# A router's gate in pairs of tiles, its statistics in the scan before it, and eight key projections moved

## The chip, the cores and the metric

The kernel runs on one core of a Trainium2 chip. A core has five engines that each work through a list of instructions in order and wait for each other on semaphores: TensorE (PE; its weight loads are shown apart as PEld), VectorE (DVE), ScalarE (ACT), GpSimd (POOL) and SyncE (SP, which here only issues transfers). Data lie in SBUF, with 128 partitions; matmuls write to eight banks of PSUM; transfers between SBUF and the large memory run on 16 DMA engines. The metric is the device time of one execution in microseconds (us).

## The reference

Four sequences of 512 tokens with 512 features (`x`) and a context of 256 features pass through four stages, each added to `x`:

```python
x = x + ssm(ctx, layernorm(x))       # selective scan over the context, gated by silu of the normed x
x = x + moe(layernorm(x))            # 64 experts, 8 chosen per token
x = x + xattn(layernorm(x), ctx)     # 16 heads; queries from x, keys and values from ctx
x = x + bitlinear_ffn(layernorm(x))  # ternary weights, 8-bit activations
```

The change concerns the scan's end, the router of the experts, and the attention's keys. The router and the keys are

```python
probs = softmax(xn @ gate_weight.T)                 # 2048 tokens x 64 experts
top_val, top_idx = top_k(probs, 8)                  # first 4 primary, last 4 secondary
# experts that are only ever secondary are replaced by a similar primary one
mapping = where(replace, best_primary, arange(64))
...
k = rmsnorm((ctx @ Wk).reshape(B, 512, 16, 128), gk)
```

The keys depend on the context alone, so their 64 tasks (4 sequences x 16 heads) can be done at any time before the attention.

## The kernel before

The 2048 tokens are 16 tiles of 128 (`NT` = 16); four tiles (`NC` = 4) are one sequence b. `x_all` stays in SBUF all the time. The program has three parts, one after the other.

**The recurrence** (`ssm_phase`). `seq` has 128 slots: b, then feature chunk c (4), then pairs of states i (8). In a slot, POOL makes `dBu` two slots ahead (`inputs(q + 2)`, three buffers), ACT makes the decay `dA` one slot ahead (in PSUM, apart from two slots per sequence that `ahead_ends` makes early in SBUF), DVE runs the scan over 1024 columns (L534), and the product with `cb` (L535) is on POOL for i = 0, 2, 4 and on DVE for the others. PE transposes the products into `yT`. In the slot with i = 2, `result` gates the previous chunk (DVE, L574) and POOL adds it to `x_all` (L576). While sequence b is scanned, `ahead` and `ahead_ends` prepare b + 1; in the last sequence there is nothing to prepare. Value projections and part of the key tasks fill PE (`values`, `key_steps`). For each sequence `stats` and `norm` (L388 to L401) compute the layernorm of that stage.

**The experts' part** (`moe_phase`) starts with `route`. Steps are put into a `Plan` with hand-set times; `run` emits them in order of time, and each engine executes its own in the order of emission. For each tile: `stats` (DVE bn_stats and bn_aggr, then four POOL instructions, L158 to L167), `norm` (ACT, L174, and a store of `xn` to memory, SP), `turn` (four PE transposes, L181), `take` (ACT copy, L186). For each pair of tiles: `logits` (eight PE instructions, L193), `turn_logits` (ACT copy L199, two PE transposes L202), `exps` (DVE maxima L207, ACT exponentials L212). Then per tile `mask` (DVE: top 8, marks; SP stores z) and `count` (PE, L909 and L914). After all tiles: `mapping` (DVE), `remap`, `ranks`, `code` and `decode` for each half of the tiles, `onehots` and `tokens` for each tile (DVE, ACT, PE), `to_places`. `PACE` = 2.7 gives each tile its place in the plan. The tiles of one pool share SBUF with tiles of pools that are closed, so a first use can wait for the last reader of what lay there.

Then `Experts.run` works through 64 experts (blocks of at most 352 rows, largest first): POOL issues the gathers of rows and weights two experts ahead, PE transposes the rows, multiplies by the gate and up weights (L1235) and the down weights (L1259 to L1269). `key_tasks` has a list of key tasks that are done one per expert from the third expert on, and `slot_tasks` and `Ternary.tasks` put other work between.

**The attention and the last stage** (`attend`) read what the others left in memory.

A key task (`Keys`) is `task` (four PE instructions of 128x512), `evict` (ACT: squares L1144 and a scaled copy L1145, SP stores the copy), `squares` (eight PE matmuls with one column, L1155) and `take` (ACT, L1167, SP stores 2 KB). Before the change the recurrence does tasks of all sequences, the experts 17, the attention 16:

```python
left = [(b, h) for b in (2, 3) for h in (6, 7)] + [(1, h) for h in range(3, H)]   # L1352
```

`load` in `Keys` brings `Wk` for eight heads to the tile `k_w` with two transfers of 512 KB, into the place that is called "hid" in the pool `late`.

Of the kernel before, what the change touches and what calls it, by code (L numbers as in the profile page):

```python
# [29 lines left out]
P = 128  # L30
# [3 lines left out]
CTX = 256  # L34
# [102 lines left out]

class Gate:
# [5 lines left out]
    def __init__(self, cm, x_all, w, dr, const, work, turned, psum):  # L144
        self.cm, self.x_all, self.dr = cm, x_all, dr
        self.work, self.turned, self.psum = work, turned, psum
# [8 lines left out]
    def stats(self, t):  # L155
        nc = self.nc
        sts = self.work.tile([P, 6], F32, name="g_st")
        nc.vector.bn_stats(sts, self.x_all[:, t, :])  # L158
        mv = self.work.tile([P, 2], F32, name="g_mv")
        nc.vector.bn_aggr(mv, sts)  # L160
        ve = self.work.tile([P, 1], F32, name="g_ve")
        nc.gpsimd.tensor_scalar(ve, mv[:, 1:2], EPS, None, ALU.add)
        rstd = self.work.tile([P, 1], F32, name="g_rstd")
        nc.gpsimd.tensor_tensor(rstd, ve, self.cm.half, ALU.pow)
        nmr = self.work.tile([P, 1], F32, name="g_nmr")
        nc.gpsimd.tensor_tensor(nmr, mv[:, 0:1], rstd, ALU.mult)
        nc.gpsimd.tensor_scalar(nmr, nmr, -1.0, None, ALU.mult)  # L167
        self.s[t] = rstd, nmr

    def norm(self, t):  # L170
        nc = self.nc
        rstd, nmr = self.s[t]
        xn = self.s[t] = self.work.tile([P, DM], F32, name="g_xn")
        nc.scalar.activation(xn, self.x_all[:, t, :], AF.Identity, bias=nmr, scale=rstd)  # L174
        nc.sync.dma_start(self.dr["xn"][t * P:(t + 1) * P, :], xn)
# [20 lines left out]
    def turn_logits(self, t):  # L196
# [3 lines left out]
        pl = self.s["pl"] = self.turned.tile([P, 2, E], F32, name="g_pl")  # L200
# [31 lines left out]
def ssm_phase(ctx, cm, x_all, w, kv, dr):  # L232
# [393 lines left out]
    def key_bank(shape, name):  # L626
        return ps.tile(shape, F32, name=name, tag=keys.banks[name == "kpss"])

    keys = Keys(cm, w, kv, small, lambda n: pool[1].tile([P, S], F32, name=f"k_{n}",
                                                         tag={"sq": "e", "kT": "wt"}[n]),  # L630
# [84 lines left out]
    for q, (b, c, i) in enumerate(seq):  # L715
# [21 lines left out]
        if i == late:  # L737
            gate(b, c)
        if q % 8 == 2 and q + 8 < len(seq):
            load_wv(q // 2 + 4)  # L740
# [32 lines left out]
def moe_phase(ctx, cm, x_all, w, kv, dr, out):  # L773
# [18 lines left out]
    with ExitStack() as es:  # L792
        more = es.enter_context(tc.tile_pool(name="b_more", bufs=1))
        keys = Keys(cm, w, kv, es.enter_context(tc.tile_pool(name="b_small", bufs=2)), None, None,
                    None)
# [1528 lines left out]
```

## Time and profile before

| | |
|---|---|
| runs (us) | 2739.28, 2743.82, 2743.28; median 2743.28 |
| profiled execution (us) | 2741.18, of which the instructions' span is 2738.4 |
| mean granted PE clock | 0.957 of full |
| busy of the span | PE 92%, DVE 55%, ACT 45%, POOL 43% |

| stage | from, to (us) |
|---|---|
| recurrence, to the last addition to `x_all` | 0 to 577.1 |
| gate of the 16 tiles: first norm, to the start of mapping | 581.5 to 649.1 |
| mapping to the first rows on PE | 649.1 to 697.8 |
| experts | 697.8 to about 1453 |
| attention and last stage | to 2738.4 |

The profile is of one execution. Its page gives the busy time of each engine, the same in 40 equal slices, the DMA queues, and the chain of work that ended last, followed back from the last instruction. Further views are asked from the trace: windows (busy time of each engine in a stretch, with the number of instructions in brackets and the granted PE clock, where 1.00 is full speed), waits (who waited for whom), and the timeline (start, duration, engine, line, operation, output<-inputs, and in square brackets the idle time before, with what ended it). PEclk in tenths and windows show the clock that was granted to PE, not a share of use.

### The profile page before, as it was taken

The page shows a single profiled execution, that of the slowest core. Times are in us where ns is not written, and L with a number is a line of the kernel's source. Part 1 is how long each engine was busy: PE and PEld are TensorE (multiplying, and loading weights), DVE is VectorE, ACT ScalarE, POOL GpSimd, SP SyncE. Part 2 cuts the span into 40 slices and gives each one's busy share as a digit, 9 for nine tenths or more (in the row PEclk, how much of TensorE's full clock was granted, in tenths as well). Part 3 has the DMA queues.
Part 4 walks back from the last instruction along what each step waited for, and adds up shares of the span by engine and source line. Part 5 has one row for each costly group of instructions (what it writes and reads, how often), then busy time and mean ns, then how long its engine had stood idle before and what let it go on. Part 6 is the DMA issues. An engine that isn't in the chain of part 4 may idle for free. (4 is left out here: it accounts for less than half of the span.)

```text
span 2738.4 us, 29994 instructions
## 1 busy us (share of the span) xinstructions
PE 2524.7 (92%) x10158; PEld 1429.8 (52%) x10158; DVE 1514.4 (55%) x2570; ACT 1239.3 (45%) x2355; POOL 1188.5 (43%) x1121
## 2 busy tenths in 40 slices
PE   5979797976899999999997899999999999999997
PEld 2545454643455656666674454445555554555543
DVE  5897979856332234334423555556665666554445
ACT  5666666643223322232322344444555555555543
POOL 3888888951333344444434433223332333211112
PEclk8989898987899999999998999999999999999999
DMA  6253535323556567889866443333432343222100
GB/s 245 90 194 109 196 117 180 116 85 104 183 180 201 175 211 224 268 273 342 298 223 206 122 143 113 96 94 122 127 100 77 116 127 112 70 81 64 52 31 20
DMA packets 198543, 403.11 MB, mean 147 GB/s; under 512 B 30563, under 2 KB 72099, under 8 KB 194288
## 3 DMA queue, kind: packets, MB, share of 16 engines
q1 hardware_dynamic: 155758, 247.76, 27.2%
q0 software_dynamic: 40576, 153.19, 18.0%
q8 instruction: 83, 1.36, 0.2%
q14 instruction: 76, 0.62, 0.1%
q10 hardware_dynamic: 2050, 0.18, 0.1%
HBM read 319.13 MB, written 81.92 MB: 146 GB/s over the span
## 5 line engine op out<-in xcount | busy, mean ns | idle before, releaser
L1889 DVE TENSOR_REDUCE mx<-psc 128x1 f32<-128x512 f32 x256 | 176.7, 690 | 457.5 <-PE psc L1886 453.8
L1235 PE MATMUL pg<-xT,wg 128*128 128x284 f32 (+12 forms) x1536 | 400.3, 405 | 1.6 <-ACT xT L1222 1.1
L1235 PEld LDWEIGHTS pg<-xT,wg 128*128 128x128 f32 x1536 | 282.9, 194 | 82.1 <-issue 33.6
L509 POOL TENSOR_TENSOR dBu<-bb,du 128x1024 f32<-128x1024 f32 x128 | 314.1, 2474 | 21.4 <-DVE dA L534 13.5
L1892 ACT ACTIVATE e<-psc,mx 128x512 f32<-128x512 f32 x256 | 176.1, 688 | 310.2 <-DVE mx L1889 309.9
L1886 PE MATMUL psc<-kT,qT 128*128 128x512 f32 x512 | 266.5, 602 | 1.0 <-ACT qT L1880 1.0
L1176 POOL DMA_INDIRECT xg<-xn_dram,tok x168 | 171.0, 1018 | 218.9 <-PE pt L1219 176.5
L1913 PE MATMUL po<-eT,v 128*128 128x512 f32 x512 | 234.9, 602 | 10.7 <-ACT eT L1907 10.7
L1852 PE MATMUL pq<-Wq,xnT 128*128 128x512 f32 x512 | 233.6, 599 | 0.7 <-ACT xnT L1811 0.7
L1922 PE MATMUL px<-Wo,oT 128*128 128x512 f32 x512 | 230.2, 593 | 0.0
L520 ACT ACTIVATE dA<-delta,negA 128x512 f32<-128x512 f32 x256 | 176.8, 694 | 81.1 <-DVE hc L535 71.0
L1906 PEld LDWEIGHTS pet<-ident,e 128*128 128x128 f32 x1024 | 127.1, 141 | 145.7 <-issue 118.8
L1863 POOL TENSOR_SCALAR qms<-qms 128x4 f32<-128x4 f32 x64 | 24.5, 382 | 411.3 <-DVE qms L1861 410.5
L534 DVE TENSOR_TENSOR_SCAN dA<-dA,dBu 128x1024 f32<-128x1024 f32 x80 | 182.8, 2284 | 24.1 <-POOL dBu L509 18.6
L1280 DVE COPY yo<-po 128x512 f32<-128x512 f32 x68 | 47.0, 691 | 230.6 <-PE po L1269 230.6
L540 PEld LDWEIGHTS yT<-ident,hc 128*128 128x128 f32 x1024 | 125.2, 149 | 92.9 <-issue 53.0
L540 PE MATMUL yT<-ident,hc 128*128 128x128 f32 x1024 | 140.6, 287 | 35.6 <-POOL hc L535 20.3
L1913 PEld LDWEIGHTS po<-eT,v 128*128 128x128 f32 x512 | 97.3, 192 | 139.1 <-issue 117.7
L1776 POOL DMA_INDIRECT yg<-y_dram,pos x124 | 125.4, 1011 | 87.2 <-issue 63.7
L1906 PE MATMUL pet<-ident,e 128*128 128x128 f32 x1024 | 154.5, 274 | 6.9 <-DVE e L1898 6.8
L1176 POOL DMA_INDIRECT wd<-down,widx x64 | 63.5, 993 | 215.6 <-PE po L1269 181.6
L1907 ACT COPY eT<-pet 128x512 f32<-128x512 f32 x256 | 148.2, 579 | 4.6 <-PE pet L1906 4.5
(352 smaller groups left out, 4475.6 us busy)
## 6 DMA issues: line engine op xcount, KB each, us to landing
y_dram<-yo SPq DMA_DIRECT2D x110, 256.0 KB
bb<-bc_dram SPq DMA_DIRECT2D x16, 1024.0 KB
cb<-bc_dram SPq DMA_DIRECT2D x16, 1024.0 KB
v_dram<-v SPq DMA_DIRECT2D x64, 256.0 KB
k_dram<-k_kT SPq DMA_DIRECT2D x64, 256.0 KB
Wq<-Wq SPq DMA_DIRECT2D x16, 1024.0 KB
kT<-k_dram SPq DMA_DIRECT2D x64, 256.0 KB
rk<-r_dram SPq DMA_DIRECT2D x64, 256.0 KB
```

The costliest lines, as they stand in the source:

```text
L509: nc.gpsimd.tensor_tensor(dBus[q], st[b]["bb"][i // 2][:, j:j + 2, :], st[b]["du"][c].unsqueeze(1).to_broadcast([P, 2, S]), ALU.mult)
L520: nc.scalar.activation(dAs[q][:, j, :], st[b]["delta"][c], AF.Exp, scale=negA[:, c, n:n + 1])
L534: nc.vector.tensor_tensor_scan(*flat, 0.0, ALU.mult, ALU.add)
L540: nc.tensor.matmul(yT[:, lc, :], t[:, lc * P:(lc + 1) * P], cm.ident, is_transpose=True, start=first and lc == 0, stop=last, skip_group_ch ...
L1176: nc.gpsimd.indirect_dma_start(out=t[0:n, :], out_offset=None, in_=table, in_offset=bass.IndirectOffsetOnAxis(ap=index, axis=0))
L1235: nc.tensor.matmul(pg[:, 0:n], s["wg"][:, c, m * P:(m + 1) * P], s["xT"][:, c, 0:n], start=c == 0, stop=c == NC - 1)
L1852: nc.tensor.matmul(pq.rearrange("p h d -> p (h d)"), xnTs[b * NC + i][:, c, :], s["Wq"][:, c, :], start=c == 0, stop=c == NC - 1)
L1886: nc.tensor.matmul(pscore, st[b, g]["qT"][:, h, i * P:(i + 1) * P], ks[n], start=True, stop=True)
L1889: nc.vector.tensor_reduce(mx, pscore, AX.X, ALU.max, negate=True)
L1906: nc.tensor.transpose(pt[:, kc, :], e[:, kc * P:(kc + 1) * P], cm.ident)
L1913: nc.tensor.matmul(po, v[:, kc, :], eT[:, kc, :], start=kc == 0, stop=kc == KB - 1)
L1922: nc.tensor.matmul(px, oTs[j * HG + h][:, i * P:(i + 1) * P], st[b, g]["Wo"][:, h, :], start=h == 0, stop=h == HG - 1)
```

## The change

A class `Stats` takes over the gate's statistics. Those of the first three sequences run in slots 4 to 15 of the recurrence's last sequence, one tile per slot; POOL's four instructions work on four tiles at once. The last four tiles follow at the start of `route`. The gate's loop is written out instead of planned: in one step PE turns the next pair's tiles around the logits of the pair in front, and the counts belong to the pair behind. `g_xn` gets three buffers; the turned logits get a PSUM bank of their own. The constants' casts are spread over the steps. Eight key tasks, (1, 8) to (1, 15), go from the experts to `route`: four in the loop (their scaled copy on DVE), one before mapping, one after the totals, one after the eighth `tokens`, one at the end. `keys.load` and a transfer for `k_ctx` come at the start of `route`. `ranks` sums the first half of the tiles once (`add_half`) and multiplies the sum instead of eight tiles.

```diff
+class Stats:
+    def __init__(self, cm, x_all, pool, work):
+        self.cm, self.x_all, self.work = cm, x_all, work
+        self.mv, self.rstd, self.nmr = ([pool.tile([P, NC] + more, F32, name=f"s_{n}{b}")
+                                         for b in range(B)]
+                                        for n, more in (("mv", [2]), ("rstd", []), ("nmr", [])))
+    def tile(self, t):
+        nc = self.cm.nc
+        st = self.work.tile([P, 6], F32, name="s_st")
+        nc.vector.bn_stats(st, self.x_all[:, t, :])
+        nc.vector.bn_aggr(self.mv[t // NC][:, t % NC, :], st)
+    def batch(self, b):
+        gp = self.cm.nc.gpsimd
+        mv, rstd, nmr = self.mv[b], self.rstd[b], self.nmr[b]
+        gp.tensor_scalar(rstd, mv[:, :, 1], EPS, None, ALU.add)
+        gp.tensor_tensor(rstd, rstd, self.cm.half.to_broadcast([P, NC]), ALU.pow)
+        gp.tensor_tensor(nmr, mv[:, :, 0], rstd, ALU.mult)
+        gp.tensor_scalar(nmr, nmr, -1.0, None, ALU.mult)
...
-    def stats(self, t):
-        nc = self.nc
-        sts = self.work.tile([P, 6], F32, name="g_st")
-        nc.vector.bn_stats(sts, self.x_all[:, t, :])
...
     def norm(self, t):
         nc = self.nc
-        rstd, nmr = self.s[t]
-        xn = self.s[t] = self.work.tile([P, DM], F32, name="g_xn")
-        nc.scalar.activation(xn, self.x_all[:, t, :], AF.Identity, bias=nmr, scale=rstd)
+        b, i = divmod(t, NC)
+        xn = self.s[t] = self.rows.tile([P, DM], F32, name="g_xn")
+        nc.scalar.activation(xn, self.x_all[:, t, :], AF.Identity,
+                             bias=self.stats.nmr[b][:, i:i + 1],
+                             scale=self.stats.rstd[b][:, i:i + 1])
         nc.sync.dma_start(self.dr["xn"][t * P:(t + 1) * P, :], xn)
...
-        pl = self.s["pl"] = self.turned.tile([P, 2, E], F32, name="g_pl")
+        pl = self.s["pl"] = self.psum.tile([P, 2, E], F32, name="g_pl")
...
-    keys = Keys(cm, w, kv, small, lambda n: pool[1].tile([P, S], F32, name=f"k_{n}",
-                                                         tag={"sq": "e", "kT": "wt"}[n]),
+    keys = Keys(cm, w, kv, cm.k_small, lambda n: pool[1].tile([P, S], F32, name=f"k_{n}",
+                                                              tag={"sq": "e", "kT": "wt"}[n]),
                 key_bank, lambda b: (st[b]["ctx"], DC - 1))
...
+        if b == B - 1 and NC <= q % SL < NC * B:
+            t = q % SL - NC
+            router_stats.tile(t)
+            if t % NC == NC - 1:
+                router_stats.batch(t // NC)
...
-        keys = Keys(cm, w, kv, es.enter_context(tc.tile_pool(name="b_small", bufs=2)), None, None,
-                    None)
+        keys = Keys(cm, w, kv, cm.k_small, None, None, None)
...
+    p3 = ctx.enter_context(tc.tile_pool(name="r_p3", bufs=3))
...
+    casts = []
     def made(name, shape, pattern, mult=0, dtype=F32):
-        t = iota(shape, f"{name}_i", pattern, mult, long=name == "bias")
-        plan.at(plan.now + 5, cast, t, name, dtype)
+        casts.append((iota(shape, f"{name}_i", pattern, mult, long=name == "bias"), name, dtype))
...
     sim = cp.tile([E, E], F32, name="sim")
+    router = Gate(cm, x_all, w, dr, cp, p2, p3, pt2, pl1, router_stats)
     nc.sync.dma_start(sim, w["similarity"])
-    router = Gate(cm, x_all, w, dr, cp, p2, pt2, pl1)
+    k_ctx = cp.tile([P, CTX // P, S], F32, name="k_ctx")
+    nc.sync.dma_start(k_ctx, w["ctxT"][:, S:2 * S].rearrange("(k p) s -> p k s", p=P))
+    keys.load(H // 2, H, late, "hid")
+    keys.row = lambda n: cp.tile([P, S], F32, name=f"k_{n}")
+    keys.psum = lambda shape, name: pl1.tile(shape, F32, name=name, tag="k")
+    keys.ctx = lambda b: (k_ctx, 0)
+    heads = list(range(H // 2, H))
+    def some_key():
+        keys.task(1, heads.pop(0))
...
+    half_sum = cp.tile([P, E], F16, name="half_sum")
+    def add_half():
+        with nc.allow_low_precision("whole numbers up to 8"):
+            vec.tensor_reduce(half_sum, chosen[:, 0:HALF, :].rearrange("p t e -> p e t"), AX.X, ALU.add)
...
-        for t in range((h + 1) * HALF - 1):
-            n = min(HALF, (h + 1) * HALF - 1 - t)
-            pe.matmul(pr[:, HALF - n:, :], c["ones"], bmid(chosen[:, t, :], n), start=False,
-                      stop=t == (h + 1) * HALF - 2, skip_group_check=True)
+        if h == 1:
+            pe.matmul(pr, c["ones"], bmid(half_sum, HALF), start=False, stop=False,
+                      skip_group_check=True)
+        for i in range(HALF - 1):
+            pe.matmul(pr[:, i + 1:, :], c["ones"], bmid(ch[:, i, :], HALF - 1 - i), start=False,
+                      stop=i == HALF - 2, skip_group_check=True)
...
         def equal(name, numbers, made, n):
-            o = p2.tile([P, SL // 2, n, 2], F16, name=name)
+            pool, tag = (p3, "g_xn") if name == "ol" else (p2, "g_xT")
+            o = pool.tile([P, SL // 2, n, 2], F16, name=name, tag=tag)
...
-    PACE = 2.7
-    for t in range(NT):
-        at = PACE * t
-        for name, d in (("stats", 0), ("norm", 2.3), ("turn", 3), ("take", 4.1)):
-            plan.at(at + d, getattr(router, name), t)
-        if t % 2:
-            for name, d in (("logits", 4.8), ("turn_logits", 6.8), ("exps", 7.6)):
-                plan.at(at + d, getattr(router, name), t)
-
-        at = PACE * (t | 1) + t % 2
-        plan.at(at + 8.6, mask, t)
-        plan.at(at + 9.6, count, t)
-        if t % HALF == HALF - 1:
-            plan.at(at + 9.7, take_mask, t // HALF)
-    T = PACE * (NT - 1) + 10.6
...
+    ones()
+    likes()
+    made("e", [P, E], [[1, E]])
+    made("lane", [P, 1], [[0, 1]], 1)
+    made("tok", [P, NT], [[P, NT]], 1)
+    before()
+    made("bias", [1, HALF, E], [[0, HALF], [1 << LOW, E]], 0, BF16)
+    rows_16()
+    lanes_16()
+    for t in range(NT - NC, NT):
+        router_stats.tile(t)
+    router_stats.batch(B - 1)
+    def ahead(name, t):
+        if t < NT:
+            getattr(router, name)(t)
+    def counts(t):
+        count(t)
+        count(t + 1)
+        if t % HALF == HALF - 2:
+            take_mask(t // HALF)
+    for t in range(2):
+        ahead("norm", t)
+        ahead("turn", t)
+    for t in range(2):
+        ahead("take", t)
+        ahead("norm", t + 2)
+    for t in range(0, NT, 2):
+        ahead("turn", t + 2)
+        keys.squares()
+        router.logits(t + 1)
+        keys.take()
+        ahead("take", t + 2)
+        ahead("norm", t + 4)
+        ahead("turn", t + 3)
+        router.turn_logits(t + 1)
+        ahead("take", t + 3)
+        router.exps(t + 1)
+        ahead("norm", t + 5)
+        if t in (4, 6, 8, 10):
+            some_key()
+        if t > 0:
+            counts(t - 2)
+        mask(t)
+        mask(t + 1)
+        keys.evict(vec)
+        if t == 10:
+            lanes()
+        elif casts:
+            cast(*casts.pop(0))
+    keys.squares()
+    keys.take()
+    counts(NT - 2)
+    assert not casts
+    def key_ends():
+        keys.squares()
+        keys.take()
+    T = 0
+    plan.at(T + 0.6, some_key)
+    plan.at(T + 0.6, keys.evict)
     plan.at(T + 0.7, mapping)
+    plan.at(T + 3.9, key_ends)
     for h in range(2):
         plan.at(T + 4 + h * 0.7, remap, h)
         plan.at(T + 6 + h * 1.5, ranks, h)
         plan.at(T + 7.5 + h * 2.5, code, h)
         plan.at(T + 9 + h * 2.5, decode, h)
+    plan.at(T + 6.1, add_half)
     U = T + 10.5
     plan.at(U + 1, totals)
+    plan.at(U + 1.1, some_key)
+    plan.at(U + 1.1, keys.evict)
...
+    plan.at(U + 1.8 * 7 + 3, some_key)
+    plan.at(U + 1.8 * 7 + 3, keys.evict)
+    plan.at(U + 1.8 * 9 + 3, key_ends)
     plan.at(U + 1.8 * NT + 4, to_places)
+    plan.at(U + 1.8 * NT + 5, some_key)
+    plan.at(U + 1.8 * NT + 5, keys.evict)
+    plan.at(U + 1.8 * NT + 5, key_ends)
...
         self.nc.scalar.activation(sq, pk, AF.Square)
-        self.nc.scalar.activation(kT, pk, AF.Copy, scale=self.cm.gkq)
+        if vec is None:
+            self.nc.scalar.activation(kT, pk, AF.Copy, scale=self.cm.gkq)
+        else:
+            vec.tensor_scalar(kT, pk, self.cm.gkq, None, ALU.mult)
...
-    left = [(b, h) for b in (2, 3) for h in (6, 7)] + [(1, h) for h in range(3, H)]
+    left = [(b, h) for b in (2, 3) for h in (6, 7)] + [(1, h) for h in range(3, H // 2)]
...
+    cm.k_small = ctx.enter_context(tc.tile_pool(name="k_small", bufs=2))
+    stats = Stats(cm, x_all, keep, cm.k_small)
```

## The prediction

> **What bounds the kernel now.** The page's slices first: TensorE (PE) is busy nine tenths nearly everywhere, except in the first eight slices and around the ninth and tenth. Its chain of waits names PE for 40% of the span but starts only at 1456 us, after everything that the change touches, so I read the stages from a table of windows (columns: busy us of PE, its weight loads, DVE, ACT and POOL, with counts; granted PE clock; DMA share; GB/s).
>
> ```profile
> 577.00:649.00 72.00, 45.83 (x176) 26.71 (x176) 31.78 (x152) 29.99 (x64) 23.97 (x107) 0.71 0.22 81
> 649.00:698.00 49.00, 27.27 (x196) 17.51 (x195) 36.07 (x95) 20.17 (x19) 7.96 (x7) 0.74 0.29 97
> 698.00:721.00 23.00, 21.55 (x82) 14.03 (x82) 3.65 (x6) 6.78 (x12) 14.29 (x15) 0.83 0.71 230
> 721.00:1450.00 729.00, 709.16 (x3201) 453.35 (x3199) 252.03 (x462) 211.16 (x463) 277.00 (x275) 0.98 0.73 235
> ```
>
> In the gate loop (577 to 649) no engine is full and the clock is 0.71: latency bounds it. From 649 to 698 DVE leads. The experts (721 to 1450) are bound by PE: 709 of 729 us at clock 0.98. The recurrence's last batch is another matter:
>
> ```profile
> 490.00:510.00 20.00, 19.63 (x103) 13.01 (x102) 17.86 (x11) 14.24 (x27) 20.00 (x10) 1.00 0.54 157
> ...
> 508.05 2.30 DVE L534 TENSOR_TENSOR_SCAN dA<-dA,dBu 128x1024 f32<-128x1024 f32 x1 [1.82 <-POOL dBu L509]
> ```
>
> POOL is busy 20.00 of 20 us, and DVE waits for it once per eight slots (26.7 us), for 1.8 us. POOL is the bound there, DVE has hardly any room. The list of waits in the gate loop (engine, line and releaser; us, times, longest):
>
> ```profile
> DVE g_nmx L207 <- PE g_pl L202: 32.9, 8, 8.0
> ...
> PEld g_pt L181 <- ACT g_xn L174: 20.8, 9, 6.6
> ...
> ACT g_lT L199 <- PE g_plT L193: 17.0, 6, 3.3
> ```
>
> Each pair of tiles is one chain in which all engines wait in turn, 8.2 us per pair.
>
> **Part 1, statistics into the recurrence: +8 us.** Twelve tiles get their statistics in slots 4 to 15 of the last batch. A tile costs DVE 0.80 us (spacing of the statistics at L158: 578.82, 579.65, 580.45), a batch four POOL instructions. The trace has these four-wide forms in the earlier batches (L396 to L401): 0.32 + 1.11 + 0.29 + 0.26 = 2.0 us, because the power on four columns takes 1.04 us where one column takes 0.57. Three batches are 6.0 us on a POOL without room. POOL also waits: batch 0 stands behind dBu at 492.84 but needs the statistics of slot 7, which follow three others (2.4 us late), so it starts at 494.4; likewise 0.5 us at the third batch. 6.0 + 1.6 + 0.5 = 8.1 us; dBu and the products hc on POOL queue behind it, and the scans wait for them. DVE's 9.6 us lie partly in its waits and otherwise run while POOL is late, so I add none. Lower end 5.9 (no waits), upper 12, for this reason:
>
> ```profile
> 397.63 2.32 POOL L401 TENSOR_SCALAR nmr<-nmr 128x4 f32<-128x4 f32 x1
> ```
>
> The same instruction took 0.26 us in batch 0. [...] the scan beside it (397.64 to 399.92) has its decay in SBUF, one that `decays(early=True)` made. [...] `ahead_ends` makes no early decays in the last batch, the decays are in PSUM, and the rows from 490 to 570 show both engines together undisturbed. I take 8.1.
>
> **Part 2, the start of the gate: normalising begins 3.0 us later than before.** Before, DVE waited 3.0 us for the store of k_ms, whose place the first statistics tile took, then the chain statistics, POOL, ACT led to the first norm at 581.49. Now batch 0's numbers are ready and k_ms has a place of its own; ACT is free after its last instruction of the recurrence (ends 576.05), +8.1, +0.3 for one cast: 584.45. The last four tiles' statistics (3.4 us of DVE, 2 of POOL, behind the constants made on POOL, some 4 us) are needed only by norm 12. SP now has k_ctx and two k_w loads, 1.5 MB, ahead of the first xn store; at 150 to 230 GB/s that is 6.5 to 10 us. Three g_xn buffers instead of two mean that norm 3 is the first to wait, and its transpose stands behind the logits; I charge nothing, up to 3 us.
>
> **Part 3, the loop.** Rows: a turn's four transposes 0.45 us at full clock, 0.9 at half; eight logits instructions 0.213 each or 0.427:
>
> ```profile
> 593.88 3.17 PE L193 MATMUL g_plT<-g_xT,gwT 128*64 128x256 f32 x8 [0.20 <-ACT g_xT L186]
> ```
>
> This one starts at half clock and speeds up at its end. In the new order the logits stand beside the next pair's turns and the counts of the pair behind. PE from one pair of turned logits to the next, full clock: counts 0.45, turn 0.45, logits 1.7, then to ACT's lT and back (0.2 + 0.37 + 0.2; the second turn lies inside), turned 0.33: 3.7. ACT: from lT to exps 1.63, norm 0.7, cast 0.2, take 0.5, norm 0.7: 3.7. I take 4.0. A pair with a key task is longer: its four matmuls take 1.72, counts and turn 0.9, but the squares share the key's PSUM bank, so they wait for both evictions, and DVE's stands behind two masks: 0.5 to the maxima, 0.55 exps, 2.36 for the masks (592.00 to 594.36), 0.69: 4.2 us. Then squares 0.95, logits 1.7, the way to ACT and back 1.1: 7.95. First pair 8.6 from the first norm, three short steps, four with a key, 4.0 for the last masks and counts: 8.6 + 12 + 31.8 + 4.0 = 56.4 us at full clock, against 67.6 now (581.49 to mapping at 649.12).
>
> The clock is the unknown. [...] The recurrence, where ten or so transposes per slot stand among projections, has clock 1.00 with PE busy 19.6 of 20 us; the stretch 225 to 325, 83% busy, has 0.90; the old loop, 64%, 0.71. The new loop is 80 to 85% busy. By the rows that is near 0.9, worth +3 us: 59.4. [...] all at half clock, short steps are 6.3, key steps 10.85 (the DVE wait then hides), in sum 76. I take 59.4: mapping starts at 643.9, **5.2 us earlier**, with four keys done.
>
> **Part 4, mapping to experts: -0.6.** The second half of the ranks had fifteen matmuls and now has eight:
>
> ```profile
> 657.99 4.28 PE L979 MATMUL pr<-chosen,ones 128*128 128x512 f16 x15
> ```
>
> Like the first half's seven (1.70 us) and one more (0.43): 2.2 us less, in front of `code(1)`, which DVE waited 2.28 us for. The half sum fits into DVE's wait. The key before mapping lies in PE's 3.96 us without work: matmuls, two evictions on ACT and squares end about when the map does; +0.5, up to 2.2 at half clock. The key after the totals falls before ACT's second ot: nothing. The one after tokens 7 costs: its eviction stands in ACT's queue before ot 9 and waits for the key, ACT comes 2.6 us late, and with two ob buffers DVE stalls on the eleventh: +2.1, and +0.2 for its squares. The last one lies in the 3.8 us of the row gathers (+0.3) and leaves PE warm, so the first eight gate_up matmuls take less than their 4.52 us (the later ones 2.53): -1.5. Wk and k_ctx for the experts now load beside those gathers; needed at the third expert, 15 us on: nothing, up to 2.
>
> **Part 5, experts: -21.8.** Eight of seventeen tasks go.
>
> ```profile
> 721.15 1.93 PE L1135 MATMUL pk<-k_ctx,k_w 128*128 128x512 f32 x4
> ...
> 727.50 1.05 PE L1155 MATMUL kpss<-ones,k_sq 128*128 128x1 f32 x8
> ```
>
> By starts (the next matmul at 722.92 and 728.41) that is 1.8 + 0.92 = 2.72 us of PE each, with nothing to take its place: DMA stands at 0.5 to 0.75 there, and ACT loses 1.3 us per task. 8 x 2.72 = 21.8; 17 if gathers take over now and then, 25 because after some squares the next gate_up ran at half clock (3.62 instead of 2.19 at 872). Wk's upper half is loaded again, unhurried.
>
> **Sum.** -5.2 - 0.6 - 21.8 = -27.6. The profiled execution took 2741.18 us (span 2738.4): 2713.6. The median of the runs shown, 2743.28, lies 2.1 higher, so 2715.7 from there. I say **2714**.
>
> **Rivals.** (a) PE's clock stays at half in the loop: +16.6, 2731. For it the 0.71 of now; against it the density. (b) The experts are really paced by gathers (DVE and POOL wait long for PE there, which speaks against it): the 21.8 fall away, 2736. (c) Better: POOL loses 5.9, the loop is warm throughout, the experts give 25: 36 less, 2706, with luck 2700. (d) Slower: SP holds. It issues in order, and the k_w loads go into space that the recurrence used; while they wait, no xn store leaves, and from norm 3 on each us is the loop's. Slack is about 4 us, so it decides from a hold of 32 us; at 40 us the result is 2751. Nothing in the row of SP (the old loads left at once at 568.56) suggests so much. (e) The loop does not overlap, each engine waiting as before, 8.2 us per pair with the four keys on top: 8.2 x 8 + 11 = 77, like (a).
>
> **Chances.** Main case 0.62 (own range 2706 to 2724), (a) and (e) 0.16, (b) 0.07, (c) 0.11, (d) 0.04. Range 2700 to 2733. A measurement tells 0.2% (5.5 us) from no change: faster 0.92, same 0.04, slower 0.04.
>
> **What would show it.** The last scan 6 to 9 us later; first norm near 584; steps of about 4 us, and 8 with a key, at clock 0.85 or more; mapping near 644; a stall of DVE after the key in the tokens; experts 2.7 us shorter each from the eleventh to the eighteenth, none elsewhere. Wrong if the scans' end stays at 571, if mapping comes after 655, or if these experts keep their length.

## The result and the profile after

The changed kernel takes 2720.99 us, the median of five executions (2710.77 to 2722.01), beside 2743.28 for the kernel before: a ratio of 0.9913, 95% interval 0.9894 to 0.9933, 22.3 us less. In a later comparison it came to 0.9927 (0.9912 to 0.9942). Below, 0.992 of about 2740 us stands for it, the mean of the two. The profiled execution took 2716.06 us (span 2714.3, mean granted clock 0.960).

First the windows by stage (busy us of PE, its weight loads, DVE, ACT, POOL with counts; granted PE clock; DMA share; GB/s): the gate's loop, mapping to experts, the experts' start, the experts.

```profile
586.00:647.50 61.50, 48.10 (x222) 27.88 (x220) 25.14 (x132) 30.48 (x69) 5.92 (x39) 0.86 0.38 133
647.50:696.00 48.50, 35.33 (x230) 21.92 (x229) 37.13 (x96) 24.72 (x30) 7.11 (x7) 0.83 0.22 79
696.00:719.00 23.00, 19.39 (x73) 12.93 (x73) 2.43 (x4) 6.03 (x11) 13.92 (x15) 0.78 0.89 271
719.00:1430.00 711.00, 691.18 (x3122) 442.90 (x3121) 253.67 (x465) 200.91 (x442) 277.94 (x276) 0.99 0.74 239
```

The loop's clock rose from 0.71 to 0.86 and PE is busy for 78% of it; it still is not full. The list of waits in the loop (586 to 648) says what is left:

```profile
DVE g_nmx L219 <- PE g_pl L214: 26.4, 7, 5.5
...
ACT g_xn L184 <- DMA xn_dram<-g_xn: 5.2, 1, 5.2
...
PE kpss L1255 <- DVE k_kT L1245: 4.8, 4, 1.8
```

DVE still waits for PE, and two waits are new: one of 5.2 us for a store, and four for a key's scaled copy. The ranks shrank as planned. The timeline of PE has one matmul of the half sum and seven others in the second half:

```profile
657.85 0.64 PE L1008 MATMUL pr<-half_sum,ones 128*128 128x512 f16 x1
658.28 1.70 PE L1011 MATMUL pr<-chosen,ones 128*128 128x448 f16 x7
```

Stage by stage, from the trace of this kernel and of every version tried below. "Mapping" is DVE's first `diag`; the experts run from the first gate_up matmul to the end of the last down matmul; all in us.

| version | ratio to before (95%) | last scan starts | last scan to mapping | mapping to gate_up | experts | after them |
|---|---|---|---|---|---|---|
| before | 1 | 568.5 | 80.6 | 52.7 | 751.3 | 1285.3 |
| changed | 0.9913 (0.9894 to 0.9933) | 578.3 | 69.2 | 54.8 | 729.7 | 1282.3 |
| changed, again | 0.9927 (0.9912 to 0.9942) | 579.3 | 68.9 | 55.8 | 733.4 | 1285.0 |
| 1 no loop keys | 0.9880 (0.9864 to 0.9895) | 577.9 | 49.2 | 57.5 | 746.3 | 1284.9 |
| 2 squares behind | 0.9888 (0.9873 to 0.9902) | 576.1 | 59.8 | 54.7 | 735.5 | 1278.6 |
| 3 copy between masks | 0.9897 (0.9874 to 0.9920) | 576.1 | 63.0 | 56.0 | 732.0 | 1281.6 |
| 4 loads in pieces | 0.9886 (0.9871 to 0.9900) | 578.8 | 62.6 | 55.5 | 733.5 | 1278.3 |
| 5 power last | 0.9926 (0.9910 to 0.9943) | 575.7 | 67.7 | 56.2 | 735.8 | 1278.4 |
| 6 statistics in waits | 0.9875 (0.9851 to 0.9898) | 568.2 | 69.4 | 54.8 | 733.0 | 1286.2 |
| 7 no routing keys | 0.9897 (0.9875 to 0.9920) | 576.7 | 44.2 | 50.0 | 751.5 | 1285.2 |
| 8 half sum alone | 1.0003 (0.9991 to 1.0014) | 572.9 | 83.3 | 50.4 | 756.8 | 1282.4 |
| 9 all mended | 0.9855 (0.9840 to 0.9869) | 570.4 | 57.2 | 55.3 | 733.7 | 1284.5 |
| 10 mended, no loop keys | 0.9870 (0.9855 to 0.9884) | 571.6 | 48.6 | 55.0 | 740.9 | 1282.6 |
| 11 mended, no routing keys | 0.9868 (0.9854 to 0.9882) | 571.9 | 45.9 | 50.0 | 751.1 | 1285.4 |

The columns also show how far one profile can be trusted. Identical code gave a last scan at 576.1 to 579.3 (changed twice, 1 to 4, 7) and 1278 to 1286 after the experts. The two middle columns repeat better where the code is the same, within about 1.5 us, apart from the 57.5 of version 1 and from the loop of before, which took 80.6 and, in version 8, 83.3. So a stage says more than a total, but 2 us in one profile say little by themselves.

### The profile page after: what moved, and what is told of

The parts are those of the page before. It is cut to its first block, busy times and chain, and to the rows that moved or that the text cites. A ratio compares the mean times of both kernels' runs of the same rounds, so it can differ in the third digit from the quotient of the medians.

```text
span 2714.3 us, 29922 instructions
## 1 busy us (share of the span) xinstructions
PE 2519.8 (93%) x10151; PEld 1428.1 (53%) x10151; DVE 1519.0 (56%) x2575; ACT 1234.1 (45%) x2351; POOL 1175.4 (43%) x1073
## 3 DMA queue, kind: packets, MB, share of 16 engines
q1 hardware_dynamic: 156574, 249.33, 27.6%
## 5 line engine op out<-in xcount | busy, mean ns | idle before, releaser
L1963 POOL TENSOR_SCALAR qms<-qms 128x4 f32<-128x4 f32 x64 | 24.8, 388 | 413.2 <-DVE qms L1961 412.4
```

## The experiments

### What a key in the loop costs

In the changed kernel a step with a key looks like this on PE (timeline: start, duration, engine, line, operation; in brackets the idle time before and what ended it):

```profile
604.13 0.33 PE L214 MATMUL g_pl<-ident,g_lT 64*128 64x64 f32 x2
604.39 1.98 PE L1231 MATMUL pk<-k_ctx,k_w 128*128 128x512 f32 x4
...
608.41 1.05 PE L1255 MATMUL kpss<-ones,k_sq 128*128 128x1 f32 x8 [1.10 <-DVE k_kT L1245]
609.39 3.61 PE L205 MATMUL g_plT<-g_xT,gwT 128*64 128x256 f32 x8
...
613.52 0.33 PE L214 MATMUL g_pl<-ident,g_lT 64*128 64x64 f32 x2
```

From one pair of turned logits to the next it is 9.39 us, where the step before has 3.65. Of the 5.7 us between them the key's matmuls and squares are 2.9. The rest is the wait of 1.10, and the logits, which take 3.61 instead of 1.94.

**1, no loop keys.** Keys (1, 8) to (1, 11) go back to the experts.

```diff
-    heads = list(range(H // 2, H))
+    heads = list(range(H // 2 + 4, H))
-        if t in (4, 6, 8, 10):
-            some_key()
-    left = [(b, h) for b in (2, 3) for h in (6, 7)] + [(1, h) for h in range(3, H // 2)]
+    left = [(b, h) for b in (2, 3) for h in (6, 7)] + [(1, h) for h in range(3, H // 2 + 4)]
```

> The four keys of the loop, (1, 8) to (1, 11), go back to the experts; all else as in the changed kernel. Theory (a key in the loop adds about 9.0 - 3.65 = 5.4 us to its step, through the wait for its evictions and the half clock after its one-column matmuls): all steps become about 3.7, mapping starts about 21 us earlier (near 626 instead of 647.5), the experts get 4 x 2.7 = 10.8 longer, net 10.5 faster than the changed kernel, near 2710 on the medians. Rival 1 (the keys keep TensorE dense, without them the clock falls towards the 0.71 of before): short steps get 5 us, the loop gains only 10 or 11, net 0. Rival 2 (the keys fill holes of the loop, as meant): the loop gains under 6, net 5 to 10 slower.

Mapping starts at 627.07. The stretch from the last scan to it is 19.8 us shorter than in the changed kernel (49.2 against 69.05, the mean of its two executions). The experts are 13 us longer than the 733.3 that the eight executions with nine tasks there average (7.6 in version 10, which has as many tasks). The total is 0.4% (11 us) below 0.992. From the second on the steps take 3.2 to 3.8 us, apart from the one that makes the lanes (4.87), so the density rival falls. So does the one of filled holes: four keys cost the loop 20 us and save the experts about 11 (2.75 each, worked out below).

**2, squares behind the logits.** The eight one-column matmuls no longer stand in front of the next pair's logits.

```diff
-        keys.squares()
         router.logits(t + 1)
-        keys.take()
+        keys.squares()
...
         router.turn_logits(t + 1)
+        keys.take()
```

> In the loop a key's eight one-column matmuls stand behind the next pair's logits instead of in front of them. Theory (in a key's step TensorE waits 0.8 to 1.8 us for kT on DVE, and the logits then run at half clock): the wait goes or moves behind the logits, the logits take 1.94 again; a key's step falls from 9.0 to about 6.5, the loop is 8 to 10 us shorter. Rival 1 (only the wait goes, the clock stays low after the one-column matmuls wherever they are): 3 to 5 us. Rival 2 (DVE with its masks is what paces a key's step): 0 to 2 us.

The timeline of PE of this version:

```profile
602.96 0.34 PE L214 MATMUL g_pl<-ident,g_lT 64*128 64x64 f32 x2
603.23 1.98 PE L1231 MATMUL pk<-k_ctx,k_w 128*128 128x512 f32 x4
...
606.07 1.94 PE L205 MATMUL g_plT<-g_xT,gwT 128*64 128x256 f32 x8
607.94 1.05 PE L1255 MATMUL kpss<-ones,k_sq 128*128 128x1 f32 x8
...
609.42 0.33 PE L214 MATMUL g_pl<-ident,g_lT 64*128 64x64 f32 x2
```

A key's step is 6.46 us, the squares lie in the time of ACT's lT, and PE has no gap: all four key steps are 6.45 to 6.46. The stretch to mapping is 9.2 us shorter, as the theory said.

**3, the copy between the masks**, which takes away only the wait.

```diff
         mask(t)
-        mask(t + 1)
         keys.evict(vec)
+        mask(t + 1)
```

> In the loop DVE makes a key's scaled copy between the two masks instead of behind both; the squares stay in front of the logits. This parts the two costs of a key's step, the wait and the clock. Theory A (the wait of 0.8 to 1.8 us is what lets the clock fall): without it the logits behind the squares take 1.94 and a key's step about 6.9, the loop is 7 to 8 us shorter. Theory B (the one-column matmuls[...] are enough): the wait goes, the logits still take 2.5 to 3.6, a key's step is about 7.9, the loop 4 us shorter.

```profile
601.70 0.34 PE L214 MATMUL g_pl<-ident,g_lT 64*128 64x64 f32 x2
...
605.42 1.05 PE L1255 MATMUL kpss<-ones,k_sq 128*128 128x1 f32 x8 [0.55 <-DVE k_kT L1245]
606.40 1.94 PE L205 MATMUL g_plT<-g_xT,gwT 128*64 128x256 f32 x8
...
608.86 0.33 PE L214 MATMUL g_pl<-ident,g_lT 64*128 64x64 f32 x2
```

Halving the wait (0.55 to 0.61 in three steps) brought the logits back to 1.94, and these steps to 7.16 to 7.22; the stretch to mapping is 6 us shorter, between the two theories. Behind eight one-column matmuls and a wait of 0.6 us the clock stayed at 1.00 here, so Theory B falls for this place; elsewhere half clock followed a stretch with sixteen of them, as the last section shows. But the third key still waits 1.79 us, and its logits also take 1.94, so the length of the wait alone does not decide either. That is taken up in the last section.

### The loads ahead of the stores

In the changed kernel ACT's norms (two rows) and SP's transfers (SPq: start, issue time):

```profile
578.49 1.52 ACT L184 ACTIVATE g_xn<-x_all,s_nmr,s_rstd 128x512 f32<-128x512 f32 x2
...
593.20 0.81 ACT L184 ACTIVATE g_xn<-x_all,s_nmr,s_rstd 128x512 f32<-128x512 f32 x1 [5.21 <-DMA xn_dram<-g_xn]
```

```profile
579.35 0.57 SPq L914 DMA_DIRECT2D k_ctx<-ctxT  x1
...
584.71 0.38 SPq L1222 DMA_DIRECT2D k_w<-Wk  x1
...
586.15 0.50 SPq L1222 DMA_DIRECT2D k_w<-Wk  x1
586.70 11.21 SPq L187 DMA_DIRECT2D xn_dram<-g_xn  x6
```

Norms 0 and 1 are done at 580.0, but their stores leave at 586.7, behind two loads that went into space of the recurrence and were issued only at 584.7 and 586.2, and then they run beside those loads, at a DMA share of 0.95 from 587.0 to 592.0. Norm 3 needs norm 0's buffer and runs at 593.2.

**4, loads in pieces.** `load_ctx` brings k_ctx behind the first four stores, `load_wk` one half of Wk each.

```diff
-    nc.sync.dma_start(k_ctx, w["ctxT"][:, S:2 * S].rearrange("(k p) s -> p k s", p=P))
-    keys.load(H // 2, H, late, "hid")
...
+    load_ctx()
     for t in range(0, NT, 2):
...
         ahead("norm", t + 5)
+        if t in (0, 6):
+            load_wk(t // 6)
```

> k_ctx is loaded behind the first four stores of xn, the first half of Wk after the step t = 0, the second half after t = 6. Theory (norm 3 waits 5.2 us because its buffer's store stands behind 1.5 MB of loads): the wait of g_xn for the store goes, the first turned logits come at about 591 instead of 595.5, mapping 4 to 5 us earlier, the total 4 to 5 us less. Rival (the store itself takes that long to land, or a later norm or the first key waits in its place): the wait appears at norms 6 or 7 or at the first key, total within 1.5 us of the changed kernel.

The first stores leave at 579.97 and norm 3 runs at 588.46 without a wait. The first turned logits come 12.4 us after the last scan starts instead of 17.2, 4.9 us sooner. The stretch to mapping is 6.5 us shorter, and the rest of the gain comes with the clock: the second pair's logits take 1.94 instead of 3.00, and the four key steps 34.8 us in all instead of 36.0, though their waits for the copy stayed (1.1 to 1.8 us). No other norm and no key waits in its place; the total is 0.34% (9 us) below 0.992.

### The statistics in the recurrence

**5, power last.** DVE keeps its statistics in slots 4 to 15; POOL's three batches come behind the last `dBu`.

```diff
             router_stats.tile(t)
-            if t % NC == NC - 1:
-                router_stats.batch(t // NC)
+        if q == len(seq) - 2:
+            for n in range(B - 1):
+                router_stats.batch(n)
```

> The statistics on DVE stay in slots 4 to 15, but the three batches on POOL (the power and the scaling) come in the slot before the last, behind the last dBu. Theory (the recurrence's +8.2 is POOL's work and its two waits): the last scan comes 8 us earlier (570 instead of 578), the statistics of 12 tiles on DVE cost nothing; at the start the constants and the norms come 0 to 2 us later against the scans, total 6 to 8 us less. Rival (DVE has no room, its 9.6 us of statistics delay the scans): the last scan comes at most 3 us earlier.

The theory failed. The last scan starts at 575.7, 1.9 us before the mean of the seven executions with the statistics as changed (577.6, from 576.1 to 579.3), so that even the 1.9 are hardly clear of their spread, and the total is that of the changed kernel. The waits from 462 to 568, first of the kernel before, then of this version, suggest why (engine, line and releaser; us, times, longest):

```profile
DVE dA L534 <- POOL dBu L509: 7.4, 4, 2.0
```

```profile
POOL hc L547 <- DVE hc L546: 3.5, 2, 2.0
...
POOL dBu L521 <- DVE dA L546: 2.3, 2, 2.0
DVE dA L546 <- POOL dBu L521: 2.1, 2, 1.2
```

Before the change DVE waited 7.4 us for POOL in this stretch and POOL for nobody. Now POOL waits 5.8 us for DVE. With POOL's part gone, DVE's twelve statistics, 9.6 us where its waits were 7.4, set the pace.

**6, statistics in waits.** In pairs before the scan with i = 5, where DVE waited in every eight slots, and four at the end.

```diff
-        if b == B - 1 and NC <= q % SL < NC * B:
-            ...
+        if b == B - 1 and i == 4:
+            router_stats.tile(2 * c)
+            router_stats.tile(2 * c + 1)
+        if q == len(seq) - 2:
+            for n in range(2):
+                router_stats.batch(n)
...
+    for t in range(2 * NC, 3 * NC):
+        router_stats.tile(t)
+    router_stats.batch(2)
     result(B - 1, NC - 1)
```

> Eight tiles' statistics come in pairs at the one place per eight slots where DVE waited for dBu before the change (before the scan with i = 5), the other four at the end of the recurrence, where DVE waits for TensorE; POOL's batches come behind the last dBu. Theory (DVE and POOL are both full in the last sequence, so that either one's statistics alone cost nearly the whole 8 us, and moving POOL's alone brought 2): the last scan comes at 569 to 571, as before the change (568.5), 7 to 8 us earlier than in the changed kernel; the total is 5 to 7 us less than the changed kernel's. Rival (something else in the last sequence changed, the key's k_ms, or a new place in SBUF): the last scan stays at 574 or later.

Last scan at 568.2, and 570.4 to 571.9 in versions 9 to 11, which have the same statistics: 570.5 on average, as without them (568.5 and, in version 8, 572.9). Eight tiles cost nothing that shows in these gaps, and of DVE's 7.4 us of waits 1.1 are left, so that 6.3 us took the eight tiles' 6.4:

```profile
DVE dA L546 <- POOL dBu L521: 1.1, 4, 0.4
```

The four at the end did not lengthen the stretch to mapping either (69.4 against 69.05). The total is 0.45% (12 us) below 0.992, more than expected, though its interval is 6 us to either side.

### What the rest is worth

**7, no routing keys**: no key and no load in `route` at all (edit as in 1, for eight heads).

> All eight keys and their loads go back to the experts; the loop, the statistics and the half sum stay as in the changed kernel. Theory: no loads before the first stores, so norm 3 does not wait; mapping starts near 622 (25 us earlier than in the changed kernel); from mapping to the first gate_up matmuls 50.5 us (52.7 before the change, less 2.2 for the ranks) against 54.8 with four keys: four keys there cost 4.3 of the 10.8 that they save later; the experts are 21.6 us longer. In all 7 to 8 us faster than the changed kernel: the eight keys as placed lose time. Rival (moved keys pay, as the forecast had it): 8 to 12 us slower than the changed kernel.

The stages came as expected: mapping at 620.9, then 50.0 us to gate_up, experts 751.5. The ratio, 0.9897, is 6 us below 0.992 where 7 to 8 were expected, but its interval reaches to 0.992, so the total by itself does not settle that the eight keys as placed lose time. The stages do: against the means of the changed kernel's two profiles, 24.8 us less to mapping, of which 4.9 are the loads' (version 4), and 5.3 less to gate_up, for 19.9 more in the experts.

**8, half sum alone**, in the kernel before.

```diff
+        if h == 1:
+            pe.matmul(pr, c["ones"], bmid(half_sum, HALF), start=False, stop=False,
+                      skip_group_check=True)
-        for t in range((h + 1) * HALF - 1):
-            ...
+        for i in range(HALF - 1):
+            pe.matmul(pr[:, i + 1:, :], c["ones"], bmid(ch[:, i, :], HALF - 1 - i),
+                      start=False, stop=i == HALF - 2, skip_group_check=True)
```

> The kernel before with the half sum of the ranks alone. Theory: code(1) waits 2.28 us less for the second ranks, but DVE's sum of 0.5 us comes before: from mapping to the first rows 1.5 to 2.2 us less, and the total 1 to 2.2 us less, hardly to be told from no change. Rival: 0, the decode of the first half or the totals are late next.

From mapping to gate_up 50.4 us instead of 52.7, so 2.3 us are gained there; versions 7 and 11, with the half sum and no key in this stretch, have 50.0 twice. The ratio, 1.0003, has an interval of 3 us to either side and cannot show it; the profile of this execution is longer than that of before, for its recurrence, gate loop and experts took 4.3, 2.7 and 5.5 us more with the same code.

### The three edits together

> The changed kernel once more, as the measure for the three versions beside it. Its ratio to the kernel before should be 0.9913 again, within 0.002; its last scan should come within 2 us of 577 and its stretch from last scan to mapping within 2 us of 69.2 (the stages before and after it vary by 2 to 4 us from one execution to another).

The ratio (0.9927) and the stretch (68.9) came as expected; the last scan, at 579.3, missed by 0.3 us.

**9, all mended**: edits 2, 4 and 6.

> Three edits together: statistics in DVE's waits and POOL's batches last, key loads in pieces, squares behind the logits; all eight keys stay in the routing. Theory (the three costs stand on the path one behind the other and add up): last scan 8 us, norm 3's wait 5 us, four keys 4 x 2.55 = 10.2 us; from last scan to mapping about 55, in all 23 us less than the changed kernel, ratio to before about 0.983. Rival (they overlap, as the two parts of the statistics did): 12 to 16 us less.

0.9855 beside 0.9927 for the changed kernel in the same comparison: 20 us, not 23, but past the rival's 12 to 16. It is 1.45% (39 us in medians) faster than the kernel before and the fastest of all that were tried. The timelines of DVE and POOL show a wait that would account for the missing 3 us:

```profile
577.11 0.67 DVE L586 TENSOR_TENSOR yg<-yT,gzT 128x512 f32<-128x512 f32 x1
582.83 0.69 DVE L151 BATCH_NORM_STATS2 s_st<-x_all 128x6 f32<-128x512 f32 x1 [5.05 <-POOL x_all L588]
...
586.04 0.26 DVE L219 TENSOR_REDUCE g_nmx<-g_pl 128x2 f32<-128x128 f32 x1
```

```profile
580.79 0.75 POOL L868 IOTA lin<- 128x256 int16 x1
581.52 1.27 POOL L588 TENSOR_TENSOR x_all<-x_all,yg 128x512 f32<-128x512 f32 x1
```

yg is ready at 577.8, but POOL adds it at 581.5, behind the third batch and the constants. DVE's statistics of the last four tiles wait for that, and the first pair's maxima stand behind them: its turned logits are there at 583.3, its maxima come at 586.0. The first two steps take 6.3 and 5.4 us instead of the 4.1 each of version 4, 3.4 us in all. A next edit would put that addition in front of the constants; it was not tried.

**10 and 11**: with the statistics as in 6, four keys outside the loop (their loads after t = 2 and t = 6), or none in the routing.

> Statistics as in the version before; the four loop keys go back to the experts, the other four stay between mapping and experts and their loads come after the steps t = 2 and t = 6. Theory (a key in the loop with its squares behind costs 2.65, as much as among the experts): last scan to mapping 45 to 46, mapping to the first gate_up 55 to 57, experts 744; the total within 2 us of the version with all eight keys kept. Rival (a loop without keys leaves room that pays elsewhere): 5 us less than that one.

> Statistics as in the two versions before; all eight keys with the experts. Theory (four keys between mapping and experts cost 4.8 us and save 4 x 2.5 = 10): last scan to mapping 45 to 46, mapping to the first gate_up 50, experts 752 to 754; 4 to 6 us slower than the two others, about 18 us less than the changed kernel. Rival (the early loads slow the experts' start as much as the keys save): no slower than the two others.

Both came out slower than version 9, by 4 us in the ratios and 2.6 and 4.5 us in the medians, but the intervals overlap, so the order of the three is not settled. Last scan to mapping came to 48.6 in version 10, for the same wait for x_all (5.04 us). A loop key with its squares behind costs 2.8 us where it saves 2.75, which is worth nothing. Four keys between mapping and experts cost 5.5 us (55.5 on average against 50.0) and saved 10.2 (740.9 against 751.1). Only the stages show this: version 11 was expected to be 4 to 6 us slower than version 10, and the ratios of the two, 0.9868 and 0.9870, do not differ.

## Why the prediction was right, and where it was not

The direction, the main case and the range (2700 to 2733) held, and short steps of 3.65 us at a mean clock of 0.86 put rivals (a) and (e) out. The sum was -27.6, and -22.3 was measured. Parts 1, 3 and 5 were near in size and right in mechanism, but for one reason in Part 1; Part 2 began from a wrong order, whose gain hid half of its mis-sized term, and Part 4 had the wrong sign. By parts:

**Part 1** (+8.1): measured +6.9 (577.6 against 570.7, the means of seven and two executions); POOL's batches took 2.0 us each and waited 1.66 and 0.65 for the statistics. The size was right and a reason wrong: "DVE's 9.6 us lie partly in its waits and otherwise run while POOL is late, so I add none". In version 5 DVE alone costs about 5 of the 6.9 (575.7 against 570.7; one profile, where equal code moves by 3 us). Two engines were nearly full (before the change POOL was busy for 84.00 and DVE for 75.62 of the 84 us from 480 to 564), and taking POOL's load away left DVE's (78.01 and 79.92 in version 5). The slow form from which the forecast made its upper end (2.32 us at 397.63) did not appear: POOL's last instruction of each batch took 0.23 us.

**Part 2**: "I charge nothing, up to 3 us" for the loads ahead of the stores is the term that was mis-sized: 4.9 us by version 4. The forecast's own figures, 6.5 to 10 us of loads against a slack of about 4, would have given 2.5 to 6. It is rival (d) in small, a hold of SP's queue of 7 us where 32 would have been needed to turn the result. The start itself was wrong the other way: normalising began 3.0 us earlier than before (578.49 against 581.49), not 3.0 later. The forecast let ACT finish the recurrence first, but in the trace norms 0 and 1 run before ACT's last instructions of the recurrence (582.16 to 585.76). That these two errors gave half of each other back was luck: the first turned logits came at 595.5 against 593.05 in the forecast.

**Part 3**: short steps 4.0, measured 5.0, 3.65 and 3.2, in sum the 12 of the forecast. Key steps 7.95 plus 3 us for the clock, in all 34.8; measured 9.39, 9.11, 9.64 and 7.86, in all 36.0; the wait for the copy was in the forecast, the logits at half clock were not but for the 3 us (and the parts of its 4.2 for DVE add up to 4.1). The clock of 0.9 "by the rows" was 0.86. In these two profiles mapping came 1.6 us earlier instead of 5.2; 2.5 of the difference are Part 2's, 1.2 the keys'. By the means used below it came 6.0 earlier, so the difference is no larger than the spread of single profiles. All at half clock, short steps would have been 6.3 by the forecast's estimate; the one of 3.65 ran at clock 1.00 (600.5 to 604.1).

**Part 4** (-0.6): +2.9, taking all versions with four keys there (55.5 on average against 52.7). The ranks gave their 2.3 us (version 8). The keys were mis-sized: with none in this stretch it takes 50.0 (versions 7 and 11), so they cost 5.5, not the 1.6 of the forecast. Set beside version 7, the changed kernel is 1.7 us late at the first matmul of the map (5.7 against 4.0 after mapping), for the first key's four matmuls took 3.38 us at a mean clock of 0.58 (647.5 to 650.9) where 0.5 were booked and "up to 2.2" allowed; it is 3.1 late at the last tokens (44.8 against 41.7), so the key among them cost 1.4, less than the 2.3 booked; and it is 4.7 late at gate_up (54.8 against 50.0). The last 1.7 stand where -1.2 was booked, and were 1.4 to 4.3 in the other versions with this key. There the key's store and 1.5 MB of loads for the experts' keys leave from 695.7 to 698.8, beside the gathers of rows, and the DMA share is 0.89 where it was 0.71; the forecast had "nothing, up to 2" for these loads. No version parts the key from them. The gain of 1.5 that the last key was to bring at the first gate_up did not come: behind this wait for rows its eight matmuls took 5.06 us instead of 4.52, at clock 0.50 (701.8 to 706.5) where it was 0.56:

```profile
647.50 3.38 PE L1231 MATMUL pk<-k_ctx,k_w 128*128 128x512 f32 x4
...
700.82 0.88 PE L1319 MATMUL pt<-ident,xg 96*128 96x96 f32 x4 [1.34 <-DMA xg<-xn_dram,tok]
702.26 5.06 PE L1335 MATMUL pg<-xT,wg 128*128 128x352 f32 x8 [0.57 <-ACT xT L1322]
```

**Part 5** (-21.8): four executions with 17 tasks took 751.1 to 756.8 in the experts (mean 752.7), eight with nine tasks 729.7 to 735.8 (733.3): -19.4. The eight experts that lost a task, the eleventh to the eighteenth, show the price itself. They took 125.8 us in all four executions with the tasks and 101.6 to 106.6 (mean 103.8) without: 22.0 less, 2.75 a task, as forecast. Windows over these eight, before and in the changed kernel:

```profile
855.31:981.16 125.85, 122.35 (x563) 75.47 (x562) 30.40 (x54) 38.85 (x89) 39.78 (x41) 0.97 0.60 185
858.55:961.76 103.21, 99.72 (x467) 61.34 (x466) 29.72 (x53) 26.58 (x64) 39.14 (x40) 0.98 0.64 205
```

PE is busy for 97% of both, gathers did not take over, and rival (b) is out. The rest of the stage, from which no task was taken, was 2.6 us longer on average; the first ten experts alone move by as much with equal code (153.5 to 156.3).

In sum 6.9 - 12.9 (last scan to mapping, 69.05 against the 81.9 of before and version 8) + 2.9 - 19.4 = -22.5. What the forecast never did was to set its own two prices side by side: a key in the loop at 7.95 - 4.0 = 3.95 us, against 2.72 among the experts. It booked the experts' gain and the loop's cost in different parts, and so did not see that four of the eight keys lose time where they stand. They cost 5.0 us each (19.8 for four in version 1).

## What to carry to other kernels

When work is moved, compare its price at both places, with the waits that its neighbours get, before adding up stages. Where two engines are both nearly full, unloading one may show little until the other is unloaded too (1.9 us of 6.9 here); look for the slot in which the fuller one waits, and put the new work there. A large load that waits at the head of a queue is paid by the small store behind it (4.9 us here), so issue it in pieces behind the stores that free a buffer.

## What the chip showed beside

**The clock changed on a grid.** In half-microsecond windows of the changed kernel, with the place inside a window worked out from its mean, PE's clock goes from 1.00 to 0.50 at 592.3, 609.4, 619.6 and 629.9, and back at 599.1, 612.8, 623.0 and 633.3. All eight lie within 0.1 us of a grid of 3.42 us (592.3 + 5 x 3.42 = 609.4, + 12 x 3.42 = 633.3). Two-microsecond windows of this kernel show one such stretch:

```profile
608.00:610.00 2.00, 1.59 (x10) 1.38 (x11) 0.36 (x1) 0.50 (x2) 0.13 (x2) 0.85 0.51 184
610.00:612.00 2.00, 2.00 (x6) 1.03 (x5) 0.00 (x0) 0.86 (x2) 0.13 (x2) 0.50 0.18 55
612.00:614.00 2.00, 2.00 (x10) 1.07 (x9) 0.11 (x1) 0.74 (x2) 0.00 (x0) 0.80 0.21 77
```

In the three key steps the half clock begins 1.0 to 2.2 us after the pause is over, at the next line of the grid, and PE is busy for all of the 3.4 us that it lasts. The four grid windows of this loop that were followed by half clock held 2.1 to 2.3 us of pause and one-column matmuls together; one with just under 2.0 us (the third key of version 6) was followed by 1.00. So was version 3's wait of 1.79 us: reckoned in steps of 3.42 from that version's own change back to 1.00 at 597.0, a line falls at 620.9, just before the wait's end at 621.0, so that the wait and the squares lie in two windows. So a wait of 1.78 us went with logits of 2.58 us in the changed kernel and of 1.94 in version 6 (the third key of each), and one of 1.10 with 3.61; and half clock followed windows in which PE was busy for up to 2.3 of 3.42 us.

Two grid windows at the end of the recurrence, of version 9 and of version 11, hold no matmuls but transposes and one-column ones. Each is shown with the window that follows it (columns as in the first table of windows):

```profile
575.87:579.28 3.41, 2.83 (x24) 2.45 (x22) 1.84 (x5) 2.13 (x6) 1.75 (x5) 1.00 0.40 132
579.28:582.69 3.41, 2.81 (x15) 1.78 (x16) 0.00 (x0) 3.17 (x6) 3.41 (x4) 1.00 0.48 160
```

```profile
576.12:579.53 3.41, 3.19 (x30) 3.04 (x29) 3.06 (x9) 1.63 (x5) 1.32 (x7) 1.00 0.46 163
579.53:582.94 3.41, 2.88 (x13) 2.15 (x13) 0.00 (x0) 2.53 (x5) 3.24 (x6) 0.50 0.33 115
```

By the spacing of starts the first holds 1.8 us of transposes, 1.0 of one-column matmuls (eight) and 0.6 of pause, and the clock stays at 1.00. The third holds 1.3 us of transposes, 1.85 of one-column matmuls (sixteen) and 0.2 of pause, and a window at 0.50 follows, though PE is busy for 3.19 us of 3.41. In the kernel before, a window with 1.6 us of pause and nearly all the rest transposes (613.5 to 616.9) was followed by one at 0.50. So the clock stayed up behind one window without a wide matmul, and fell behind one with twice the one-column matmuls and behind one with more pause. What sets it is not shown by three windows. In the fourth window PE works 2.7 us at transposes, and the half clock goes on to 586.4.

**The same program moves by some microseconds from one execution to another**, in the recurrence (576.1 to 579.3) and after the experts (1278.3 to 1286.2), with intervals of totals of about 5 us to either side. Here 2.3 us (version 8) could be read only from a stage.
